# A perceiver layer on one core: the opening of its cross attention, with the query weights prepared a head at a time

## The chip, the core and the metric

The kernel runs on one core of a Trainium2 chip. The core's engines work side by side, each through its own list of instructions in order: TensorE (PE in the profile; PEld are its weight loads), VectorE (DVE), ScalarE (ACT), GpSimd (POOL), and SyncE (SP), whose list here holds almost only DMA transfers. They wait for one another by semaphores. The metric is the device time of one execution in microseconds.

## The reference

One perceiver layer works on a latent array `x` of 32 sequences of 64 tokens with 512 features. It adds three blocks: a cross attention to a context of 32 x 1601 x 512, a causal self attention, and a feed-forward block with ternary weights. Only the opening of the cross attention is touched here:

```python
xn = _rmsnorm(_layernorm(x), rms_scale)              # 2048 tokens x 512
q = jnp.einsum('BTD,NDH->BTNH', xn, q_w)             # 4 heads of 128
q = _apply_rope(q, q_pos) * HEAD_DIM ** (-0.5)       # rotary positions
...
logits = jnp.einsum('BTKGH,BSKH->BKGTS', q, k)
masked = jnp.where(mem_mask[:, None, None, None, :], logits, MASK_FILL)
```

The mask marks which context rows are used. How many rows matter differs by sequence, and the kernel finds that out at run time.

## The kernel before

**Queries without a normalised x.** The kernel never forms `xn`. The weights are scaled by `1 + rms_scale` and their mean over the input features is taken off, which does the layernorm's centring; the tokens' deviations enter only after the product, as a factor per token. So `query` (L231) multiplies the raw, transposed tokens with these centred weights, and `rotate_query` (L237 to L242) multiplies by cosine and sine tables that already hold each token's inverse deviation. The 2048 tokens are taken in four groups of 512, named 0 to 3, and each group has four heads: 16 queries, named here q(group, head).

**The steps for one group.** `fetch_raw` (L194) brings the tokens row by row and `fetch_wide` (L189) brings them transposed. `spread_of` (L200, L201) takes mean and variance of 128 rows on DVE, four times; `deviations` (L207 on DVE, L208 on POOL) makes the inverse deviation. `diagonals` (L215, ACT) writes it on a diagonal; `tables` spreads it over all partitions with one matmul called rb (L224) and makes the cosine and sine tables from it (L226, L227, DVE). `query` is four float32 matmuls of 128 x 512, which the profile lists as eight records. `rotate_query` copies the two halves of the result crosswise (L237, L238, ACT) and makes two products and a sum on DVE (L240, L241, L242). L240 waits for the copies, though it reads only PSUM and a table. The copies have two buffers, so a head's copies wait for L242 of the head two before. The temporary that L240 writes is a single one, so L240 waits for L242 of the head before.

**PSUM.** A query's result lies in one of four banks. Heads 0 and 2 share one pair of banks and heads 1 and 3 the other, so that q(g+1, h) takes the bank that q(g, h) had, and may start only when L240 of that head has read it.

**Weights.** `wo` (1 MB) first holds the query weights, arranged by input chunk: `wo[:, c]` is chunk c of all four heads. They come in two transfers (L289). Four matmuls of 128 x 512 (wmean, L326) give the mean over the input features of all 512 output columns, and four DVE instructions (L346), one for each chunk, scale and centre them.

**Ranking.** Between these the kernel counts which blocks of the context each sequence uses (count, L308, and L315), ranks the sequences by need (L328 to L341, DVE), and places them in a fixed order by two small matmuls (placed, L343 and L344). L353 to L358 write the order and a flag as integers (`ints`). All engines load the flag and branch on it; the transfers of context rows (`nat`, L453) and of transposed context (`ct`, L465) are addressed by the order.

**Order.** `keep_busy(n)` (L284) issues n matmuls whose result nobody reads. At the end of each block `in_order` ties every engine's instructions to the order in which the Python code issued them, SP's transfers too. So what stands ahead in an engine's list holds up all behind it.

**Behind the branch.** `cross_last` runs groups 1 to 3 through `query_steps`; between the queries of group 2 it projects the first sequences' keys and values (kvp, L523). Everything after that (attention by pairs of sequences, self attention, feed-forward) is the same code in both kernels.

## Time and profile before

| | us |
|---|---|
| median of three runs | 894.86 (894.26 to 896.26) |
| the profiled execution | 895.05 |
| its span | 892.2 |
| PE busy in the span | 881.8 (99%) |
| DVE, ACT, POOL busy | 627.4, 377.3, 67.1 |
| first query starts | 11.43 |
| first rb matmul starts | 21.84 |
| fifth query starts | 27.13 |
| first kvp matmul starts | 45.23 |

Rows of the timeline read: start, length, engine, line, operation, tiles out and in, shape, the number of records merged, and in brackets the idle time before them and what ended it. A float32 matmul is two records for PE. Where neighbouring records overlap, the distance between their starts (the pitch) is what one costs.

### The profile page before, as it was taken

Reading aid. Unit: us, or ns where it says so; the run is one execution under the profiler, and the core shown is the slowest. Engines: PE = TensorE matmul, PEld = TensorE weight load, DVE = VectorE, ACT = ScalarE, POOL = GpSimd, SP = SyncE. Lnnn points to the kernel's source line nnn. Section 1 sums busy time; section 2 is a strip of 40 time slices with the busy share of each in tenths; the row PEclk is TensorE's granted clock in tenths of the full one; section 3 lists DMA queues with packets and bytes.
Section 4 is the critical chain, followed back from the end, with each engine's and each line's share of the span. In section 5 each row is a group of like instructions: output and inputs, shape, how many; then the busy total and the mean of one; then the engine's idle time right before and its main releaser. Section 6 shows DMA issues by size and latency. Waiting matters only on the chain.

```text
span 892.2 us, 12926 instructions
## 1 busy us (share of the span) xinstructions
PE 881.8 (99%) x4536; PEld 636.5 (71%) x4536; DVE 627.4 (70%) x1198; ACT 377.3 (42%) x811; POOL 67.1 (8%) x79
## 2 busy tenths in 40 slices
PE   9999999999999999999999999999999999999997
PEld 4456777777778767667666766676668778788885
DVE  5975656455655671588789988986866886876864
ACT  2554545555455441222232323224654554555550
POOL 0110111111101100000000000000001000010000
PEclk9999999999999999999999999999999999999999
DMA  7975798775685343011101101100000020010101
GB/s 259 329 251 179 230 258 259 220 257 157 191 259 160 108 148 116 1 48 34 39 26 47 45 27 37 48 12 1 1 1 1 1 47 1 12 37 1 34 14 53
DMA packets 58723, 88.05 MB, mean 99 GB/s; under 512 B 10516, under 2 KB 30872, under 8 KB 58264
## 3 DMA queue, kind: packets, MB, share of 16 engines
q1 hardware_dynamic: 57888, 86.58, 31.6%
q8 instruction: 38, 0.62, 0.3%
q10 hardware_dynamic: 760, 0.55, 0.2%
q14 instruction: 37, 0.30, 0.1%
HBM read 78.72 MB, written 4.19 MB: 93 GB/s over the span
## 4 chain that ended last, share of the span: by engine, by line
PE 95%; DVE 3%; ACT 1%; issue 0%; POOL 0%; ACTq 0%; POOLq 0%
PE y L1533 14%; PE kvp L523 13%; PE fh L1179 12%; PE aV L1268 6%; PE aWQ L1256 6%; PE q L231 6%; PE aWK L1256 6%; PE aout L1377 6%; PE xo L649 6%; PE lgp L565 3%; PE enc L633 3%; PE sc L1311 2%; PE po L1363 2%; PE pt L618 2%; PE aptp L1350 1%; PE ftp L1168 1%
## 5 line engine op out<-in xcount | busy, mean ns | idle before, releaser
L523 PE MATMUL kvp<-wkv,ct 128*128 128x256 f32 x576 | 134.7, 379 | 0.0
L523 PEld LDWEIGHTS kvp<-wkv,ct 128*128 128x128 f32 x576 | 107.0, 190 | 21.6 <-issue 8.8
L1533 PE MATMUL y<-wp,hTh 128*128 128x512 f32 x236 | 94.5, 400 | 0.4 <-DVE xres L1510 0.4
L1533 PE MATMUL y<-wp,hTl 128*128 128x512 f32 x236 | 92.8, 393 | 0.0
L1179 PE MATMUL fh<-fxh,wf 128*128 128x512 f32 x256 | 72.2, 403 | 1.2 <-DVE xres L1380 0.8
L1187 ACT ACTIVATE bank<-fh 128x512 f32<-128x512 f32 x64 | 38.2, 597 | 76.6 <-PE fh L1179 76.4
L1179 PE MATMUL fh<-fxl,wf 128*128 128x512 f32 x256 | 70.5, 397 | 0.0
L530 ACT ACTIVATE kv<-kvp,rstd 128x256 f32<-128x256 f32 x72 | 34.0, 473 | 84.2 <-PE kvp L523 84.2
L572 DVE CUSTOM_DVE_ANT_0 pr<-lgp,bias 128x384 f32<-128x384 f32 (+6 forms) x64 | 28.5, 458 | 46.9 <-PE lgp L565 46.6
L1377 PE MATMUL aout<-bank,aoT 128*128 128x512 f32 x128 | 59.0, 604 | 0.0
L1528 DVE SCALAR_TENSOR_TENSOR hTl<-bank,lnw,hTh 128x512 fp32r<-128x512 f32 x59 | 44.1, 751 | 21.0 <-ACT hTh L1527 20.9
L649 PE MATMUL xo<-wo,encT 128*128 128x512 f32 x128 | 57.8, 594 | 0.2 <-ACT encT L642 0.2
L231 PE MATMUL q<-xres,wo 128*128 128x512 f32 x128 | 56.4, 593 | 0.6 <-DVE wo L346 0.6
L1179 PEld LDWEIGHTS fh<-fxh,wf 128*128 128x128 f32 x256 | 46.6, 188 | 14.1 <-DVE xres L1380 1.6
L1179 PEld LDWEIGHTS fh<-fxl,wf 128*128 128x128 f32 x256 | 48.2, 188 | 11.2
L1533 PEld LDWEIGHTS y<-wp,hTh 128*128 128x128 f32 x236 | 44.3, 188 | 14.0 <-DVE xres L1510 3.4
L1195 DVE TENSOR_TENSOR sums<-sums,bank 128x512 f32<-128x512 f32 x56 | 38.5, 687 | 19.7 <-ACT bank L1187 19.7
L1533 PEld LDWEIGHTS y<-wp,hTl 128*128 128x128 f32 x236 | 44.5, 188 | 9.9
L1333 ACT ACTIVATE s<-s 128x1024 f32<-128x1024 f32 x15 | 15.9, 1059 | 84.3 <-DVE s L1326 84.3
L1268 PE MATMUL aV<-bank,axT 128*128 128x512 f32 x112 | 51.5, 602 | 0.0
L1256 PEld LDWEIGHTS aWQ<-axT,bank 128*128 128x128 f32 x224 | 42.6, 190 | 11.8 <-issue 6.7
L1355 ACT COPY wo<-aptp 64x256 f32<-64x256 f32 x64 | 23.3, 365 | 64.8 <-PE aptp L1350 47.6
(176 smaller groups left out, 1564.0 us busy)
## 6 DMA issues: line engine op xcount, KB each, us to landing
nat<-in_ctx_dram SPq DMA_DIRECT2D x64, 256.0 KB, 4.7
ct<-in_ctxT_dram SPq DMA_DIRECT2D x7, 768.0 KB, 4.5
xres<-in_x_dram SPq DMA_DIRECT2D x8, 512.0 KB, 6.1
xres<-in_x_dram SPq DMA_DIRECT2D x32, 128.0 KB, 5.0
qs<-bank SPq DMA_DIRECT2D x32, 128.0 KB, 3.8
raw_g<-in_W_fcT_dram SPq DMA_DIRECT2D x16, 256.0 KB, 4.4
raw_g<-in_W_projT_dram SPq DMA_DIRECT2D x16, 256.0 KB, 3.5
raw_q<-in_W_fcT_dram SPq DMA_DIRECT2D x16, 256.0 KB, 2.9
```

Source lines behind the costliest of these rows:

```text
L231: nc.tensor.matmul(ps, wq[:, c, h, :], wide(g)[:, c], start=(c == 0), stop=(c == DC - 1))
L523: nc.tensor.matmul(ps.rearrange("p k h -> p (k h)"), cts[p][:, c, j * P : (j + 1) * P], wkv[:, c].rearrange("p k h -> p (k h)"), start=(c ...
L530: nc.scalar.activation(kvs[p][:, j], ps, AF.Copy, scale=rstds[p][:, j : j + 1])
L649: nc.tensor.matmul(o, encT[:, h].rearrange("p s t -> p (s t)"), wo[:, h, :], start=(h == 0), stop=(h == NH - 1),)
L1179: nc.tensor.matmul(ps, wf[:, c, cols], part[:, c, :], start=(i == 0 and c == 0), stop=(i == 1 and c == DC - 1),)
L1187: nc.scalar.activation(g, ps, AF.Gelu)
L1195: nc.vector.tensor_tensor(sums[:, 0], so_far[0], g, ALU.add)
L1256: nc.tensor.matmul(ps[:, m, :], ws[w][:, c, (m0 + m) * P : (m0 + m + 1) * P], xT[:, c, :], start=(c == 0), stop=(c == DC - 1),)
L1268: nc.tensor.matmul(ps, xT[:, c, i * P : (i + 1) * P], ws["WV"][:, c, :], start=(c == 0), stop=(c == DC - 1),)
L1377: nc.tensor.matmul(ps, oT[:, c, :], ws["WO"][:, c, :], start=(c == 0), stop=(c == DC - 1))
L1528: nc.vector.scalar_tensor_tensor(lo, g, w, hi.bitcast(F32), ALU.mult, ALU.subtract)
L1533: nc.tensor.matmul(y, part[:, t, :], wp[:, c, :], start=(c == 0 and i == 0), stop=(c == FC - 1 and i == 1),)
```

## The change

The query weights are arranged by head: `wo[:, h]` holds all four chunks of head h. They arrive in three transfers (head 0, head 1, heads 2 and 3) with the transposed tokens of group 0 behind the first. The mean is taken for one head at a time, four matmuls of 128 x 128, and a head is centred by four DVE instructions of 128 x 128. Head 0 is done right after the counts, ahead of the ranking; heads 1 and 2 after q(0, 0) and the ranking's end; head 3 after q(0, 1). The filler matmuls go from 5 + 4 to 5 + 1 + 2.

The transposed tokens of group 1 are fetched at the start, instead of behind q(0, 1). The statistics of group 1 move on DVE from ahead of the tables of group 0 to behind the rotation of q(0, 1), and their diagonals on ACT from behind the copies of q(0, 1) to behind those of q(0, 2). The tables of group 1 (its rb and L226, L227) move across the branch: they were made ahead of q(1, 0) and are now made behind q(1, 2), and on DVE behind the statistics of group 2. The rotations of q(1, 0), q(1, 1) and q(1, 2) then follow together. Groups 2 and 3 keep their order.

```diff
-    wq = wo.rearrange("p c (h k) -> p c h k", h=NH)
+    wq = wo.rearrange("p h (c k) -> p c h k", c=DC)
...
         for g in range(1, GROUPS):
             more = g + 1 < GROUPS
+            waiting = []
             for h in range(NH):
-                q = query(g, h, psq(h, f"q_{g}_{h}"))
-                if h == 0 and g > 1:
+                waiting.append((h, query(g, h, psq(h, f"q_{g}_{h}"))))
+                if h == (2 if g == 1 else 0):
                     tables(g, qrot, psr(f"rb_{g}"))
-                rotate_query(g, h, q)
+                if h >= 2 or g > 1:
+                    for k, q in waiting:
+                        rotate_query(g, k, q)
+                    waiting.clear()
                 if more and h < 2:
                     spread_of(g + 1, 2 * h)
...
         nc.scalar.dma_start(scale1, a["rms"])
-        for k in (0, 2):
-            nc.sync.dma_start(wo[:, k : k + 2], a["wq"][:, k : k + 2])
-        keep_busy(5)
+        nc.sync.dma_start(wo[:, 0], a["wq"][:, 0])
+        fetch_wide(0, [nc.sync, nc.sync])
+        nc.sync.dma_start(wo[:, 1], a["wq"][:, 1])
+        nc.sync.dma_start(wo[:, 2:], a["wq"][:, 2:])
+        fetch_raw(0)
+        fetch_wide(1, [nc.sync])
+        qrot = fetch_rotations(r1)
+        nc.sync.dma_start(wkv, a["wkv"])
...
-        fetch_wide(0, [nc.sync, nc.sync])
-        fetch_raw(0)
-        qrot = fetch_rotations(r1)
-        nc.sync.dma_start(wkv, a["wkv"])
+        heads = [ps_q[h % 2].tile([P, GQ], F32, tag="q", name=f"q_0_{h}") for h in range(NH)]
+
+        def averaged(h):
+            ps = ps_b.tile([P, HD], F32, tag="b", name=f"wmean_{h}")
+            for c in range(DC):
+                nc.tensor.matmul(
+                    ps, each[:, c], wq[:, c, h], start=(c == 0), stop=(c == DC - 1)
+                )
+            return ps
+
+        def centre(h, ps):
+            for c in range(DC):
+                nc.vector.scalar_tensor_tensor(
+                    wq[:, c, h], wq[:, c, h], scale1[:, c : c + 1], ps, ALU.mult, ALU.subtract
+                )
+
+        keep_busy(5)
...
-        keep_busy(4)
-        wmean = ps_b.tile([P, D], F32, tag="b", name="wmean")
-        for c in range(DC):
-            nc.tensor.matmul(wmean, each[:, c], wo[:, c], start=(c == 0), stop=(c == DC - 1))
+        keep_busy(1)
+        centre(0, averaged(0))
+        keep_busy(2)
         need = r1.tile([B, B], F32, name="need")
...
         nc.vector.tensor_scalar(here, table[:, 2], rank, None, ALU.is_equal)
+        query(0, 0, heads[0])
         placed = ps_r.tile([P, 2, B], F32, tag="r", name="placed")
...
-        for c in range(DC):
-            nc.vector.scalar_tensor_tensor(
-                wo[:, c], wo[:, c], scale1[:, c : c + 1], wmean, ALU.mult, ALU.subtract
-            )
-        heads = [ps_q[h % 2].tile([P, GQ], F32, tag="q", name=f"q_0_{h}") for h in range(NH)]
-        query(0, 0, heads[0])
...
         nc.vector.tensor_copy(ints[:, B:], fit)
+        means = [averaged(h) for h in (1, 2)]
+        for h in (1, 2):
+            centre(h, means[h - 1])
+        query(0, 1, heads[1])
+        mean = averaged(3)
         for k in range(4):
             spread_of(0, k)
         deviations(0)
         diagonals(0)
+        centre(3, mean)
         for c in range(DC):
             nc.scalar.activation(wkv[:, c], wkv[:, c], AF.Copy, scale=scale1[:, c : c + 1])
-        query(0, 1, heads[1])
         fetch_raw(1)
-        fetch_wide(1, [nc.sync])
-        for k in range(4):
-            spread_of(1, k)
-        deviations(1)
         query(0, 2, heads[2])
         tables(0, qrot, ps_b.tile([P, GQ], F32, tag="b", name="rb_0"))
         query(0, 3, heads[3])
         for h in range(NH):
             rotate_query(0, h, heads[h])
             if h == 1:
+                for k in range(4):
+                    spread_of(1, k)
+                deviations(1)
+            if h == 2:
                 diagonals(1)
-        tables(1, qrot, ps_b.tile([P, GQ], F32, tag="b", name="rb_1"))
...
-    arrays["wq"] = given["L0_xattn_q_w"].reshape(NH, DC, P, HD).transpose(2, 1, 0, 3).reshape(P, DC, D)
+    arrays["wq"] = given["L0_xattn_q_w"].reshape(NH, DC, P, HD).transpose(2, 0, 1, 3).reshape(P, NH, D)
```

## The prediction

> **What bounds the kernel now.** I read the page's busy shares and its chain of waits first, then PE's timeline over the opening, then ACT's and DVE's.

> ```profile
> PE 881.8 (99%) x4536; PEld 636.5 (71%) x4536; DVE 627.4 (70%) x1198; ACT 377.3 (42%) x811; POOL 67.1 (8%) x79
> ...
> PE 95%; DVE 3%; ACT 1%; issue 0%; POOL 0%; ACTq 0%; POOLq 0%
> ```

> PE is busy for 99% of the span and carries 95% of the chain. So a change in the opening is worth just what it shifts PE's later work.

> ```profile
> 1.06 2.50 PE L284 MATMUL idle<-ones 128*128 128x128 f32 x10 [1.06 <-DVE neghalf L96]
> ...
> 5.02 2.08 PE L284 MATMUL idle<-ones 128*128 128x128 f32 x8
> 6.89 3.70 PE L326 MATMUL wmean<-wo,each 128*128 128x512 f32 x8
> ...
> 11.43 10.57 PE L231 MATMUL q<-xres,wo 128*128 128x512 f32 x24 [0.64 <-DVE wo L346]
> 21.84 1.02 PE L224 MATMUL rb<-xres,ones 128*128 128x512 f32 x2
> ...
> 26.16 1.13 PE L224 MATMUL rb<-xres,ones 128*128 128x512 f32 x2
> 27.13 17.40 PE L231 MATMUL q<-xres,wo 128*128 128x512 f32 x40
> 44.37 1.02 PE L224 MATMUL rb<-xres,ones 128*128 128x512 f32 x2
> 45.23 1.89 PE L523 MATMUL kvp<-wkv,ct 128*128 128x256 f32 x8
> ```

> From 11.43 on PE never stops. A query costs 3.44 us (17.40 / 5 less the last record's tail), an rb 0.86. The five queries from 27.13 run without a gap, so q(2,0) starts at 27.13 + 4 x 3.44 = 40.9. I use the start of the first kvp, 45.23, as the mark: behind it the PE list is the same in both kernels, and PE has no large idle to absorb a shift.

> What a 128-wide float32 record costs on PE is not seen in the opening, where idle records follow each other at 0.213 us; a later stretch shows it:

> ```profile
> 288.53 0.61 PE L565 MATMUL lgp<-kT,qs 128*128 128x128 f32 x4
> 288.97 1.89 PE L633 MATMUL enc<-pT,kv 128*128 128x256 f32 x8
> ```

> Four records take 288.97 - 288.53 = 0.44, so 0.110 each: PE ran the idle records at half speed, and was at full speed when wmean began (eight 512-wide records at 0.43).

> The handshake around a rotation, ACT and then DVE:

> ```profile
> 18.50 1.28 ACT L215 ACTIVATE xres<-ident,qrs 128x128 f32<-128x128 f32 x4 [14.36 <-POOL qrs L208]
> 19.68 1.69 ACT L364 ACTIVATE wkv<-wkv,scale 128x256 f32<-128x256 f32 x4
> 21.39 0.58 ACT L237 COPY qt<-q 64x512 f32<-64x512 f32 x1
> 21.98 0.58 ACT L238 COPY qt<-q 64x512 f32<-64x512 f32 x1
> ```

> ```profile
> 34.34 0.68 DVE L240 TENSOR_TENSOR xres<-q,xres 128x512 f32<-128x512 f32 x1
> 34.94 0.68 DVE L241 TENSOR_TENSOR qt<-qt,xres 128x512 f32<-128x512 f32 x1
> 35.65 0.69 DVE L242 TENSOR_TENSOR bank<-xres,qt 128x512 f32<-128x512 f32 x1
> 36.26 0.69 DVE L200 BATCH_NORM_STATS2 stats_q<-xres 128x6 f32<-128x512 f32 x1
> ```

> A rotation takes DVE 1.92 us before other work (34.34 to 36.26), and 2.12 before another rotation (24.82 to 26.94 in group 0). q(1,0) was read by 35.0; its bank is asked for at 40.9, so q(2,0) has 5.9 us to spare.

> **Step 1: the first query.** The counts stay, and one filler starts at 5.02. Its two records (0.375 and 0.213 apart, as now) put head 0's mean at 5.61. Its weights, 256 KB issued at 1.20, should have landed: 145 KB took 2.3 us and 512 KB took 4.6. Eight records at the half-speed 0.213, the last one lasting 0.42, give the mean at 7.5. Then comes an instruction that no row shows: a 128-wide scaling on DVE. Bounds: the 32-wide L331 at 0.18 us, and the 512-wide L346 at 0.74; on the line between them 0.29. PE started 0.06 after L346's first one, so q(0,0) starts at 7.5 + 0.3 + 0.06, say 7.9, against 11.43. Its tokens hold it no longer: they now stand behind 0.4 MB; before, the first half landed at 8.8 behind 1.2 MB, at 1.35 us for 512 KB, so about 6.5 now and the second half about 8.0, which is first used at 9.7. The ranking, now behind head 0's scaling, ends near 10.9 (need to here took 2.4), before q(0,0) is through at 11.4; nobody waits for it. **Gain 3.5.**

> **Step 2: what moves in among the queries.** Three means of eight records at 0.110 are 2.65, and placed 0.2 (it lay under a wait before). Three queries with what lies between took 10.41 (11.43 to 21.84). So rb(0) starts at 7.9 + 10.41 + 2.65 + 0.2 = 21.2, **0.65 earlier** than 21.84. It needs diagonals(0). On DVE the integers end at 12.4, eight scalings follow at an estimated 0.26 (pitch of L346 0.66; of a 32-wide instruction 0.10 to 0.2) with mean 1 ready at 12.6, then statistics 14.9 to 18.2 (13.88 to 17.19 took 3.31), POOL and ACT 2.6 more: 20.8. Slack 0.4; the other heads' scalings are done before their queries. The four 128-wide means cost 32 x 0.110 = 3.5, as much as the wide ones (8 x 0.43); the loss is only that 24 of these records now lie behind the first query.

> [...]

> **Step 3: group 1's tables, and DVE.** Count from T = start of rb(0). PE: q(0,3) and three queries of group 1, then rb(1), then q(1,3) want q(2,0) at T + 19.06 (as before, 40.9 - 21.84, rb(1) only moved). Now DVE. L226 starts at T + 1.05 (rb at 65.87 to L226 at 66.92), the rotation of q(0,0) at T + 2.3, of q(0,1) at T + 4.4, group 1's statistics at T + 6.3, L207 at T + 9.65, rotation of q(0,2) at T + 9.7 (q(1,2) wants that bank at T + 11.3: 0.9 to spare). Then a gap: diagonals(1) stand on ACT ahead of q(0,3)'s copies and wait for POOL. From L207: 1.31 to ACT (17.19 to 18.50), 1.18 for the diagonals, 1.17 for the copies, so rotation of q(0,3) at T + 13.35, where DVE was free at T + 11.8. Then statistics of group 2 from T + 15.3 (3.39), tables(1) 1.21, and L240 of q(1,0) from T + 19.9 to T + 20.55. q(2,0), which takes its bank, starts at T + 20.6: **PE stands still for 1.55 us**, and all queries, kvp and the rest queue behind it. Restarting costs 0.1 (first to second record 0.53 instead of 0.43). Next late is rb(2): q(1,2)'s copies wait for L242 of q(1,0) at T + 21.9, copies and diagonals(2) end at T + 24.4, rb(2) is wanted at T + 24.1: 0.3, and 0.1 for the restart. From there DVE has 13 us of work for 21 us of PE's and catches up.

> [...]

> **Queues.** SP issues one transfer more (0.43 of issue, all issued by 6, in front of nothing waiting). wide(1) goes out with the opening; wkv lands near 17 instead of 14.2, used at 20.7. raw(1) still waits for the statistics of group 0, now at 16.6 and 18.2 (before 15.38 and 16.97); it stands in front of the context rows, so the earlier integers start nothing earlier. raw(2) waits for the statistics of group 1: 29.2 and 30.9 (before 23.25 and 24.72), landing by 37, while DVE takes its first half at 36.5 and second at 38.1. wide(2) behind it goes at 31.7 and lands 7.1 later, 38.8, wanted at 40.3. ct lands near 41, wanted at 46.6. POOL only has its power instructions later.

> **Sum.** -0.65 + 1.55 + 0.1 + 0.3 + 0.1 = +1.4 us. Against the profiled execution (892.2 of span, 895.05) that is 896.45; it lies 0.2 above the median of 894.86. I take **896.4**. 0.2% (1.8 us) is about what measurement can tell from no change here.

> **Rivals.**
> *The ledger holds but for small sizes*, forecast: 895.3 to 897.5. Chance 0.48, a third of it above the 896.65 where slower begins.
> *The narrow scaling is dear* (slower). At 0.66 pitch instead of 0.26, eight of them push the statistics, diagonals(0) and rb(0) by 3.2 less the slack of 0.4, and the first query by 0.45: rb(0) near 24.1, net +4.3, 899.3. It decides from a pitch of 0.36, where it costs 0.4 and the total passes 1.8. For it: the instruction reads PSUM and is unmeasured; against: L331 is short. Chance 0.17.
> *PE cools in the stall* (slower): eight records of q(2,0) at 0.86 instead of 0.43, +3.4, 899.8. For it: the idle records show that a half speed exists; against: the 0.64 wait ahead of 11.43 left full speed. Chance 0.07.
> *No stall* (not slower): if ACT's copies of q(0,3) do not stand behind the diagonals, DVE gains 1.55 and q(2,0) starts in time: 895.05 - 0.65 + 0.1 = 894.4. With the first query at 7.4 and PE already at full speed, 893.5 to 894. For it: the gap hangs on one order on ACT; against: that order is written out. Chance 0.2, a third of it faster by 0.2%.
> *The early tokens do not come early*: first half at 8.8 as before, q(0,0) at 8.9, +1.0, 897.4. The rest, 0.08, holds this, late transfers of raw(2) and what I do not see.

> **Chances.** Faster 0.07 + 0.03 = 0.10. Within: 0.32 + 0.13 + 0.01 = 0.46. Slower 0.16 + 0.17 + 0.07 + 0.04 = 0.44. The range takes in no stall and most of the dear scaling: 894.3 to 898.9.

> **What would show it.** After: q(0,0) near 7.9; 128-wide wmean records 0.11 apart behind it; rb(0) near 21.2; a wait of PE before the ninth query, 1 to 2 us, ended by DVE L240; ACT's copies of q(0,3) waiting behind diagonals; first kvp near 46.6. It is wrong if PE shows no such wait, if rb(0) waits for ACT long, or if records behind the wait are 0.86 apart.

## The result, and the profile after

| | before | after |
|---|---|---|
| median | 894.93 us (894.26 to 896.31, 9 executions) | 898.12 us (896.83 to 899.27, 9 executions) |
| the profiled execution, and its span | 895.05, 892.2 | 898.62, 897.0 |
| first query starts | 11.43 | 8.00 |
| first rb starts | 21.84 | 21.46 |
| q(2,0) starts | 40.89 (27.13 + 4 x 3.44) | 42.49 |
| first kvp starts (the mark) | 45.23 | 47.32 |

The ratio is 1.0029, with a 95% interval of 1.0021 to 1.0037: the changed kernel is 0.29% slower (by the two medians alone 0.36%). 896.4 was forecast. The result lies inside the range and on the side on which the forecast lay, but the rise is 3.2 us and not 1.5. The mark accounts for 2.1 of it; where the rest comes from is half of what follows. The two spans differ by 4.8 us, but the last instruction that computes (a DVE sum ahead of the output transfer) starts only 3.77 later, at 890.05 instead of 886.28, and the times of the two profiled executions differ by 3.57; the spans are therefore not compared below.

From the page of the changed kernel, the chain of waits by engine:

```profile
PE 94%; DVE 3%; ACT 1%; issue 1%; POOL 0%; ACTq 0%; POOLq 0%
```

PE is still the bound (busy 884.0 us of 897.0), and the chain has a new percent of "issue": a wait of PE in which the page names no releaser. PE's timeline of the changed kernel over the opening shows it:

```profile
5.61 1.91 PE L313 MATMUL wmean<-wo,each 128*128 128x128 f32 x8
...
8.00 3.67 PE L231 MATMUL q<-xres,wo 128*128 128x512 f32 x8
...
11.81 2.05 PE L313 MATMUL wmean<-wo,each 128*128 128x128 f32 x16
...
21.46 1.02 PE L224 MATMUL rb<-xres,ones 128*128 128x512 f32 x2
22.32 13.90 PE L231 MATMUL q<-xres,wo 128*128 128x512 f32 x32
...
36.91 3.60 PE L231 MATMUL q<-xres,wo 128*128 128x512 f32 x8
42.49 3.67 PE L231 MATMUL q<-xres,wo 128*128 128x512 f32 x8 [1.98 <-issue]
46.36 1.12 PE L224 MATMUL rb<-xres,ones 128*128 128x512 f32 x2 [0.20 <-ACT xres L215]
47.32 1.89 PE L544 MATMUL kvp<-wkv,ct 128*128 128x256 f32 x8
```

The first query is 3.4 us earlier, but 16 and then 8 narrow mean records now lie behind it, 0.11 apart, and only 0.4 us is left at rb(0). Five queries and an rb further on PE stands still for 1.98 us ahead of q(2,0). The bracket says "issue"; which instruction it is comes from DVE's timeline:

```profile
34.97 0.69 DVE L240 TENSOR_TENSOR xres<-q,xres 128x512 f32<-128x512 f32 x1 [1.72 <-ACT qt L238]
...
37.09 0.69 DVE L200 BATCH_NORM_STATS2 stats_q<-xres 128x6 f32<-128x512 f32 x1
...
41.71 0.68 DVE L240 TENSOR_TENSOR xres<-q,xres 128x512 f32<-128x512 f32 x1
```

L240 at 41.71 is that of q(1,0), whose bank q(2,0) takes; it ends at 42.39, and PE starts 0.1 later. Ahead of it DVE lost 1.72 us waiting for ACT's copies of q(0,3). ACT's timeline has the reason:

```profile
32.46 1.28 ACT L215 ACTIVATE xres<-ident,qrs 128x128 f32<-128x128 f32 x4 [5.37 <-POOL qrs L208]
33.77 0.58 ACT L237 COPY qt<-q 64x512 f32<-64x512 f32 x1
```

The diagonals of group 1 stand ahead of the copies and wait for POOL, as the prediction said.

**The part that was not in the sum.** Behind the mark the two PE lists keep a distance of 2.1 us, up to the fh matmuls (a product of the feed-forward block) at 651.21 (649.08 before). Then the distance grows to 3.8 (659.19 against 655.43) and stays there to the end. PE's timeline there, first of the kernel before:

```profile
647.17 1.98 PE L1151 MATMUL spread<-side,pick 4*128 4x512 f32 x4
649.08 1.20 PE L1179 MATMUL fh<-fxh,wf 128*128 128x512 f32 x4
...
651.05 3.60 PE L1377 MATMUL aout<-bank,aoT 128*128 128x512 f32 x8
655.43 1.19 PE L1179 MATMUL fh<-fxh,wf 128*128 128x512 f32 x4 [0.79 <-DVE xres L1380]
```

and of the changed kernel:

```profile
649.30 1.98 PE L1172 MATMUL spread<-side,pick 4*128 4x512 f32 x4
651.21 1.19 PE L1200 MATMUL fh<-fxh,wf 128*128 128x512 f32 x4
...
653.67 4.73 PE L1398 MATMUL aout<-bank,aoT 128*128 128x512 f32 x8
659.19 1.20 PE L1200 MATMUL fh<-fxh,wf 128*128 128x512 f32 x4 [0.78 <-DVE xres L1401]
```

The aout row (the output product of the self attention) took 3.60 in the kernel before and takes 4.73 here. The spread row holds matmuls that use only 4 rows (4*128, 4x512; the fh and aout rows have 128*128). The view by stretches of 2 us (stretch and its length, then the busy time and instructions of PE, PEld, DVE, ACT and POOL, then the granted clock of PE, the DMA share and GB/s), again of the changed kernel:

```profile
652.00:654.00 2.00, 2.00 (x7) 1.63 (x6) 1.65 (x3) 1.04 (x3) 0.00 (x0) 0.63 0.00 0
654.00:656.00 2.00, 2.00 (x3) 0.68 (x3) 0.67 (x3) 1.14 (x2) 0.54 (x1) 0.51 0.00 0
```

PE is busy all the time, but was granted half clock from 652.54 to 655.95, for 3.41 us (the stretches before and behind have 1.00), which costs the 1.6 us by which the distance grows. The kernel before has 1.00 in each of these stretches. So two things had to be explained: the mark, and a half-clock stretch 600 us behind everything that the change touches.

The second matters for reading all times below. Executions of one kernel fall into groups some 1.6 us apart. That these are the executions with no such stretch, with one and with two is read from the profiled ones and from the size of the step; it was not seen in each. The nine of the changed kernel are 896.83, 896.98 and 897.19, then 897.51, then five from 898.12 to 899.27: by this reading its median is a time with a half-clock stretch, while most executions of the kernel before have none.

### The profile page after: what moved, and what is told of

Read it like the earlier page. It is cut to its first block, busy times and chain, and to the rows that moved or that the text cites. A ratio compares the mean times of both kernels' runs of the same rounds, so it can differ in the third digit from the quotient of the medians.

```text
span 897.0 us, 12987 instructions
## 1 busy us (share of the span) xinstructions
PE 884.0 (99%) x4558; PEld 639.4 (71%) x4558; DVE 629.3 (70%) x1210; ACT 377.3 (42%) x811; POOL 67.3 (8%) x79
## 4 chain that ended last, share of the span: by engine, by line
PE 94%; DVE 3%; ACT 1%; issue 1%; POOL 0%; ACTq 0%; POOLq 0%
PE y L1554 13%; PE kvp L544 13%; PE fh L1200 12%; PE aV L1289 6%; PE aWQ L1277 6%; PE aWK L1277 6%; PE aout L1398 6%; PE xo L670 6%; PE q L231 6%; PE lgp L586 3%; PE enc L654 3%; PE sc L1332 2%; PE po L1384 2%; PE pt L639 2%; PE aptp L1371 1%; PE ftp L1189 1%
## 5 line engine op out<-in xcount | busy, mean ns | idle before, releaser
L593 DVE CUSTOM_DVE_ANT_0 pr<-lgp,bias 128x384 f32<-128x384 f32 (+6 forms) x64 | 28.5, 458 | 46.9 <-PE lgp L586 46.6
L231 PE MATMUL q<-xres,wo 128*128 128x512 f32 x128 | 56.9, 593 | 2.0 <-issue 2.0
L1200 PEld LDWEIGHTS fh<-fxh,wf 128*128 128x128 f32 x256 | 46.6, 188 | 14.1 <-DVE xres L1401 1.6
L1200 PEld LDWEIGHTS fh<-fxl,wf 128*128 128x128 f32 x256 | 48.5, 189 | 11.3
L1277 PEld LDWEIGHTS aWQ<-axT,bank 128*128 128x128 f32 x224 | 42.6, 190 | 11.8 <-issue 6.7
L1277 PE MATMUL aWK<-axT,bank 128*128 128x256 f32 x224 | 50.6, 379 | 0.0
```

Of the source, the lines that this page charges most:

```text
L231: nc.tensor.matmul(ps, wq[:, c, h, :], wide(g)[:, c], start=(c == 0), stop=(c == DC - 1))
L1200: nc.tensor.matmul(ps, wf[:, c, cols], part[:, c, :], start=(i == 0 and c == 0), stop=(i == 1 and c == DC - 1),)
L1277: nc.tensor.matmul(ps[:, m, :], ws[w][:, c, (m0 + m) * P : (m0 + m + 1) * P], xT[:, c, :], start=(c == 0), stop=(c == DC - 1),)
```

## The experiments

All kernels compute the whole result. They ran in three sets, each set on one chip beside its own executions of the kernel before: medians 895.59 (first set, 30 executions), 895.34 (second, 32) and 895.45 (third, 27). Ratios go by these.

### The kernel before, once more

> The kernel before, run again as if it were a change, so that the mean clock of each of its executions is listed. Theory 'clock windows': 1.1 us of the 3.2 us lost lie behind the first kvp, in one window of 3.41 us at half clock (652.54 to 655.95 in the profile after); whether a window falls so depends on a phase the kernel does not set, so some executions of the kernel before must show it too: mean clock near 0.997 with times 1.7 us above those at 0.999. Rival 'the change slows the later code': every execution of the kernel before stands at 0.999, and its times do not go with its clock.

Measured: 895.0 us (12 executions), ratio 0.9993 (0.9985 to 1.0002). Ten lie between 893.9 and 895.7; the two with a mean clock of 0.997 instead of 0.999 took 896.3 and 896.6. So, going by time and mean clock together, for no profile shows one, the kernel before has executions with a slower clock too, only fewer. In its profiled execution the first query started at 10.72, rb(0) at 21.13 and the first kvp at 44.89: 0.7, 0.7 and 0.3 earlier than in the execution that the prediction was worked out from. One profile fixes the times of this opening to a few tenths only.

### Statistics of group 1 back ahead of the tables

```diff
+        for k in range(4):
+            spread_of(1, k)
+        deviations(1)
         for h in range(NH):
             rotate_query(0, h, heads[h])
             if h == 1:
-                for k in range(4):
-                    spread_of(1, k)
-                deviations(1)
-            if h == 2:
                 diagonals(1)
```

> The changed kernel, with group 1's statistics back ahead of the tables of group 0 and its diagonals behind the copies of q(0,1), as before; rb(1) stays behind three queries. Theory 'late statistics': the wait ahead of q(2,0) (2.14 us) goes. The second half of group 1's rows landed at 22.66 in the profile after, so tables of group 0 move from 22.5 to about 24.4 and q(1,0) waits about 0.6; first kvp at 45.3 instead of 47.3, time 2.1 below the changed kernel, level with the kernel before. Rival 'the narrow means cost': the time stays within 0.5 us of the changed kernel, and the kvp comes no earlier than 46.5.

Measured: 896.55 us (12 executions), ratio 1.0010 (1.0002 to 1.0019). PE's timeline:

```profile
26.55 10.54 PE L231 MATMUL q<-xres,wo 128*128 128x512 f32 x24 [0.78 <-DVE xres L240]
...
37.78 7.03 PE L231 MATMUL q<-xres,wo 128*128 128x512 f32 x16
```

There is no wait ahead of q(2,0): 16 records follow 37.78 without a gap. A smaller wait of 0.78 stands at q(1,0) instead, because DVE twice waits 0.7 for the rows of group 1 to arrive before it can take their statistics, and the rotation of q(0,0) comes late (25.61). The mark is 45.51. So the place of the statistics on DVE, with the diagonals that follow them, makes the 2-us wait. The median, expected level with the kernel before, is 0.1% above it, and one thing here is not explained: seven of the twelve executions lie 1.5 us above the others at mean clocks of 0.996 and 0.997, although the profiled one (895.06) holds no wait near 2 us. The rows of group 1 may arrive later in those; no run shows it.

### Only ACT's order changed

```diff
-            if h == 2:
+            if h == 3:
                 diagonals(1)
```

> The changed kernel, with group 1's diagonals on ACT behind the copies of q(0,3) instead of ahead of them. If ACT's order makes 1.7 us of DVE's lateness, the rotation of q(0,3) starts at 33.4 instead of 34.97, the wait ahead of q(2,0) falls from 2.14 to about 0.5, first kvp at 45.7: 1.6 below the changed kernel, 0.5 above the kernel before. If the statistics on DVE alone set it, the wait stays above 1.5 and the time within 0.6 us of the changed kernel.

Measured: 895.36 us (12 executions), ratio 1.0003 (0.9994 to 1.0011). PE's timeline, the two rows that answer to 42.49 and 47.32 above:

```profile
40.64 3.67 PE L231 MATMUL q<-xres,wo 128*128 128x512 f32 x8 [0.41 <-PE q L231]
...
45.47 1.89 PE L544 MATMUL kvp<-wkv,ct 128*128 128x256 f32 x8
```

and DVE's row of L240 of q(0,3), 34.97 above:

```profile
33.11 0.69 DVE L240 TENSOR_TENSOR xres<-q,xres 128x512 f32<-128x512 f32 x1
```

It starts earlier and has no wait ahead of it. PE's wait falls from 1.98 to 0.41 and the mark from 47.32 to 45.47. Of these 1.85 us, 0.29 is not the edit's: rb(0) is that much earlier in this execution (21.17). Counted from rb(0), one line of order on ACT, an engine that is 42% busy, is worth 1.56 us, and what is left of the slow-down lies within what can be measured.

### The order of group 1 alone, with the old front

The new `query_steps` and the new places of the statistics, diagonals and tables of group 1, put into the kernel before.

```diff
-        for k in range(4):
-            spread_of(1, k)
-        deviations(1)
...
             if h == 1:
+                for k in range(4):
+                    spread_of(1, k)
+                deviations(1)
+            if h == 2:
                 diagonals(1)
-        tables(1, qrot, ps_b.tile([P, GQ], F32, tag="b", name="rb_1"))
```

> The kernel before with the new order of group 1 alone: its statistics behind the rotation of q(0,1), its diagonals behind that of q(0,2), its tables behind three queries; weights, means and opening as before. Theory 'late statistics': the same chain from rb(0) (21.84) to q(2,0) takes 21.03 us, so q(2,0) starts at 42.9 with 2.1 us of waiting, first kvp 47.7, 2.5 us slower than the kernel before. Rival 'the opening costs': no wait longer than 0.5, first kvp within 0.5 us of 45.2, the same time as before.

Measured: 898.31 us (6 executions), ratio 1.0031 (1.0019 to 1.0043). PE's timeline:

```profile
42.69 3.67 PE L231 MATMUL q<-xres,wo 128*128 128x512 f32 x8 [1.91 <-issue]
...
47.53 1.67 PE L527 MATMUL kvp<-wkv,ct 128*128 128x256 f32 x7
```

The whole loss is there without the head-wise weights: from rb(0), at 21.30 here, to the mark it is 26.23 us, against 23.39 and 23.76 in the two profiles of the kernel before.

### The head-wise front alone

The reverse: the new front, with group 1 handled as before.

```diff
+        for k in range(4):
+            spread_of(1, k)
+        deviations(1)
         for h in range(NH):
             rotate_query(0, h, heads[h])
             if h == 1:
-                for k in range(4):
-                    spread_of(1, k)
-                deviations(1)
-            if h == 2:
                 diagonals(1)
+        tables(1, qrot, ps_b.tile([P, GQ], F32, tag="b", name="rb_1"))
...
-                if h == (2 if g == 1 else 0):
+                if h == 0 and g > 1:
                     tables(g, qrot, psr(f"rb_{g}"))
```

> The front of the change alone (query weights a head at a time, counts ahead of the ranking), with the statistics, diagonals and tables of group 1 where they were before, ahead of the branch. Theory: rb(0) near 21.4, 0.4 earlier than before; then rb(1), wanted at 25.7, waits for the diagonals of group 1, which POOL and ACT have ready near 26.9, so the fifth query starts near 28.1 instead of 27.1 and the first kvp near 46.0, 0.8 later than before: ratio 1.0005 to 1.0012. Rival (the head-wise front is a gain that the new order of group 1 throws away): rb(1) does not wait, kvp near 44.8, median 0.4 below before.

Measured: 896.13 us (11 executions), ratio 1.0009 (1.0000 to 1.0018). PE's timeline:

```profile
7.92 3.67 PE L231 MATMUL q<-xres,wo 128*128 128x512 f32 x8 [0.67 <-DMA xres<-in_xT_dram]
...
26.50 1.13 PE L224 MATMUL rb<-xres,ones 128*128 128x512 f32 x2 [0.67 <-ACT xres L215]
```

The front by itself is no gain: rb(1) waits 0.67 for the diagonals of group 1, and the mark is 45.55. A first query 3 us earlier moves rb(0) hardly at all. Over the eleven profiles of kernels with the new front, rb(0) starts between 20.93 and 21.82, on average at 21.33; the three profiles with the old front have 21.84, 21.13 and 21.30, on average 21.42.

### Filling the wait with matmuls that nobody reads

```diff
+            if g == 2:
+                fill = psr("fill")
+                for _ in range(8):
+                    nc.tensor.matmul(fill[:, :P], ones, ones, start=True, stop=True)
             for h in range(NH):
                 waiting.append((h, query(g, h, psq(h, f"q_{g}_{h}"))))
```

> The changed kernel with eight 128-wide filler matmuls put in front of q(2,0), where PE stands still for 2.1 us; nobody reads their result, the computation is the same. Theory A (the standing still itself makes the half-clock windows of 3.41 us, later in the execution, more frequent): the wait is filled, q(2,0) still starts near 42.5 and the first kvp near 47.3, but executions with a mean clock of 0.997 or less fall from 7 in 9 to about the 2 in 12 of the kernel before, and the median goes to about 897.2. Theory B (the 2 us of shift set the frequency, by where the late matmuls lie against the windows, idleness or not): the same starts and the same share of low clocks as in the changed kernel, median about 898.1.

Measured: 896.8 us (10 executions), ratio 1.0021 (1.0012 to 1.0030). PE's timeline:

```profile
39.82 1.95 PE L252 MATMUL fill<-ones 128*128 128x128 f32 x16
42.00 3.67 PE L231 MATMUL q<-xres,wo 128*128 128x512 f32 x8 [0.23 <-issue]
```

q(2,0) starts as far behind rb(0) as in the changed kernel (21.07 against 21.03): the bank is free no sooner. Yet eight of ten executions lie between 896.4 and 897.1, and only two 1.5 us above, at 898.2 and 898.7. The changed kernel has five of nine there. That is near the share that theory A expects, and the standing still would have a second price, paid by the clock. It is not proved by this: 2 of 10 against 5 of 9 are few, the two ratios' intervals overlap, by the measure that was named beforehand (a mean clock of 0.997 or less) it is 4 of 10 against 7 of 9, and the kernel with the statistics ahead of the tables has seven of twelve in the upper group without a wait near 2 us. The profile of the next run shows that the clock can fall at this wait.

### Where the clock falls: at the wait, or at the 4-row matmuls

```diff
-        pick = fw.tile([4, 2, P], F32, name="pick")
+        pick = fw.tile([P, 2, P], F32, name="pick")
...
+            nc.gpsimd.memset(side, 0.0)
             nc.vector.tensor_copy(side[:4], ps[:4])
...
-                    nc.tensor.matmul(ps, pick[:, k, :], side[:4], start=True, stop=True)
+                    nc.tensor.matmul(ps, pick[:, k, :], side, start=True, stop=True)
```

> The changed kernel with the spread matmuls near 649 us (four records of 512 columns, of which only 4 rows held data) widened to all 128 rows, the added rows zero, so that the result is the same. Theory C (a window filled by matmuls of 4 rows counts as idle, and the next one is given half clock): no half-clock window behind the spread, PE's shift against the kernel before stays at +2.1 us through 659, executions with a mean clock of 0.997 or less become rare, median about 896.9 to 897.2, that is 1.6 lower less what the wider operand costs (a memset on an engine off the path: nothing). Theory D (the window falls there by chance or for another reason): the half-clock window stays in the executions and the median is within 0.5 of the changed kernel's.

Measured: 897.11 us (11 executions), ratio 1.0023 (1.0014 to 1.0032). By the times alone it was inconclusive: five of eleven executions still lie 1.5 us above the rest. The profiled execution, one of them (898.39), showed why. Its PE timeline, and then its stretches of 2 us:

```profile
42.85 5.37 PE L231 MATMUL q<-xres,wo 128*128 128x512 f32 x8 [1.99 <-issue]
```

```profile
42.00:44.00 2.00, 1.15 (x2) 0.64 (x3) 1.97 (x4) 0.00 (x0) 0.11 (x1) 0.82 1.01 390
44.00:46.00 2.00, 2.00 (x4) 0.69 (x3) 1.86 (x4) 1.76 (x5) 0.00 (x0) 0.50 1.06 324
```

Eight records that take 3.67 behind the same wait in the changed kernel's profile take 5.37 here: PE got half clock from 43.28 to 46.69, right behind the wait. This is the rival "PE cools in the stall", in an execution of a kernel whose opening is that of the changed one. So the changed kernel can lose the clock at two places, and this run could close only the later one. The later one is told apart below, on a base without the wait.

### Half the statistics ahead of the tables

```diff
+        for k in (0, 1):
+            spread_of(1, k)
         for h in range(NH):
             rotate_query(0, h, heads[h])
             if h == 1:
-                for k in range(4):
+                for k in (2, 3):
                     spread_of(1, k)
                 deviations(1)
-            if h == 2:
+            if h == 3:
                 diagonals(1)
```

> The changed kernel with the statistics of group 1 cut in two: the first two of the four go ahead of the tables of group 0, where DVE waits for rb(0) anyway; the other two stay behind the rotation of q(0,1), and the diagonals of group 1 go behind ACT's copies of q(0,3). Theory (the shift of the mark is DVE's lateness alone, made of 3.3 us of statistics in the rotations and 1.7 us of gap by ACT's order): with half the statistics out and the gap gone, L240 of q(1,0) starts about 3.4 us earlier than in the changed kernel (near 38.3), PE does not wait before q(2,0), rb(0) stays at 21.5, the first kvp is at 44.8, 0.4 ahead of the kernel before, and the median is 0 to 0.5 below it (ratio 0.9995 to 1.000). Rival (something behind the mark, such as the late transfers of group 2's tokens, takes the gain): a new wait of PE before rb(2) or kvp of over 0.5 us, and a median over 895.5.

Measured: 894.34 us (11 executions), ratio 0.9990 (0.9981 to 0.9999). PE's timeline, the queries on both sides of q(2,0) and the mark:

```profile
36.52 7.03 PE L231 MATMUL q<-xres,wo 128*128 128x512 f32 x16
...
44.24 1.89 PE L546 MATMUL kvp<-wkv,ct 128*128 128x256 f32 x8
```

q(2,0) follows q(1,3) without a gap, and from rb(0) at 21.07 to the mark PE never waits: 23.17 us, against 23.39 and 23.76 in the two profiles of the kernel before and 25.86 in that of the changed one. L240 of q(1,0) starts at 38.16, as expected; the gain is larger than expected. The same kernel on another chip:

> The same kernel as the one with the statistics of group 1 cut in two, on another chip and as the base of the three kernels run with it. Theory (its mark is 0.4 to 0.9 ahead of the kernel before and nothing takes it back): ratio 0.999 again, interval within 0.998 to 1.000, about 2 in 11 executions some 1.5 us above the rest. If the earlier 1.0 us was that chip's chance: ratio 0.9997 to 1.0003.

Measured: 894.22 us (11 executions), ratio 0.9988 (0.9979 to 0.9997). The gain of 0.1% is there twice. It is 1.0 and 1.2 us by the medians, but 0.6 by the marks (44.24 and 44.37, against 45.23 and 44.89). The two profiled executions of the kernel before, 895.05 and 894.78, lie 0.3 to 0.7 below the medians of their kernel in these sets; in which part of it the others lose that was not shown.

### The spread matmuls, wide, twice, and both

On the kernel with the statistics cut in two: the 128-row spread of above; the 4-row spread issued twice; the 128-row spread issued twice.

```diff
+                    for _ in range(2):
-                    nc.tensor.matmul(ps, pick[:, k, :], side[:4], start=True, stop=True)
+                        nc.tensor.matmul(ps, pick[:, k, :], side[:4], start=True, stop=True)
```

> The kernel with the statistics cut in two, and the spread matmuls near 646 us widened from 4 rows to 128 (zeros in the rows added, the same result). Theory C (4-row matmuls count as idleness of PE and now and then bring a half-clock window): the 2 in 11 executions that lie 1.5 us above the rest disappear, the rest stay at 894.3, median 0 to 0.2 lower. Theory D (those executions have another cause): their share stays near 2 in 11.

> The kernel with the statistics cut in two and the spread matmuls of 4 rows issued twice (the second writes the same values over the first; the result is the same): 3.96 us of 4-row work in a row instead of 1.98. Theory C: whatever the phase, one window of 3.41 us now holds at least 2.0 us of it, so a half-clock window follows in nearly every execution, and the time is 894.3 + 2.0 + 1.6 = 897.9, in some executions 899.5 with two such windows. Theory D: 896.3, as with 128 rows, and no half-clock window behind the spread.

> The kernel with the statistics cut in two and the spread matmuls widened to 128 rows and issued twice: the same 3.96 us of PE time as with 4 rows, with all rows active. Theories C and D both: 894.3 + 2.0 = 896.3 and no half-clock window; against the 4-row kernel C expects 1.6 less, D the same. If the extra matmuls lie beside a wait that PE has anyway, both kernels gain back the same amount.

| kernel | median, us | executions, and their spread | ratio to the kernel before |
|---|---|---|---|
| 4 rows, once | 894.22 | 11: ten from 893.64 to 894.59, one 895.78 | 0.9988 (0.9979 to 0.9997) |
| 128 rows, once | 894.02 | 11: 893.72 to 894.84 | 0.9985 (0.9976 to 0.9994) |
| 4 rows, twice | 899.16 | 5: 898.94 to 899.20 | 1.0044 (1.0030 to 1.0058) |
| 128 rows, twice | 895.92 | 11: 895.41 to 896.51 | 1.0006 (0.9997 to 1.0015) |

The second pass costs 1.9 us with 128 rows, about its own time (from the first spread record to the second set of fh matmuls 4.46 us instead of 2.75), and 4.9 with 4 rows. The stretches of 2 us of the 4-row kernel, issued twice:

```profile
650.00:652.00 2.00, 2.00 (x5) 1.22 (x5) 1.18 (x4) 0.59 (x1) 0.54 (x1) 0.50 0.00 0
652.00:654.00 2.00, 2.00 (x6) 1.60 (x5) 0.00 (x0) 0.00 (x0) 0.00 (x0) 0.50 0.00 0
654.00:656.00 2.00, 2.00 (x4) 0.89 (x3) 0.00 (x0) 1.23 (x2) 0.00 (x0) 0.50 0.00 0
```

and of the 128-row kernel, issued twice:

```profile
650.00:652.00 2.00, 2.00 (x9) 1.47 (x8) 1.48 (x4) 0.59 (x1) 0.31 (x1) 1.00 0.00 0
```

## Why the prediction was right or wrong

**The bound.** Right: PE carries 94% of the chain and the mark moves the end. Behind the mark the lists kept their distance (2.1) until the clock fell.

**Step 1, the first query.** Right: 7.9 forecast, 8.00 measured; over the eleven profiles with the new front it is 7.45 to 8.36, on average 7.87, so that the agreement to 0.1 in one profile is partly luck. The scaling that no row had shown has a pitch close to 0.26 (four in 1.12, eight in 2.16), as the line between two rows gave; so the dear scaling, which had a chance of 0.17, did not come. The tokens were the weak point: their first half landed at 7.87, not 6.5. The page shows no loss by it in this execution, but in five of the eleven profiles with the new front the first query waits for that transfer, 0.6 to 1.3 us (0.67 in the front alone).

**Step 2, what moves in among the queries.** The price of the narrow means was right, 0.11 a record. The gain at rb(0) was over-sized: 0.65 forecast, 0.38 in this pair of profiles, 0.1 as an average over all. The first error is 0.1 us in the start of the first query and 0.2 in the length of the stretch. The second is that the sum was made against one execution whose rb(0), at 21.84, was the latest of three.

**Step 3, the wait.** The mechanism was right in each link: DVE's L240 of q(1,0) ends it, ACT's copies stand behind the diagonals, and rb(2) waits a little afterwards. The size was not: 1.55 was forecast, q(2,0) starts 2.14 later than the two rb and five queries ahead of it need. Counted from rb(0), PE wanted the bank at 18.89, not 19.06; the rotation of q(0,3) began at 13.51, not 13.35; statistics of group 2 at 15.63, not 15.3, since a rotation took 2.12 on DVE here where 1.92 or so was counted; and the end is at 21.03, not 20.6. Four small errors, all to the same side, make the wait 0.6 longer. The first only lengthens the wait; the other three put q(2,0) 0.43 later behind rb(0). With 0.38 instead of 0.65 from step 2 they make the mark 2.09 later instead of 1.4. That the wait belongs to the order and not to the front is shown by the order alone (mark 47.53). Of the 2.09, ACT's list carries 1.56, counted from rb(0), as the late diagonals show; so the rival "No stall", which hung on that list, had the right condition, but a wait of 0.41 would have been left.

**The rival that was put too low.** "PE cools in the stall" had a chance of 0.07 and a price of 3.4. A half-clock stretch is the part of the result for which the sum has no term; that the wait would cost none of the clock was assumed. The argument against it, that a wait of 0.64 had left full speed, was no bound for one of 2 us. Where it was seen, its price was 1.7 (5.37 instead of 3.67), not 3.4: the half clock lasted 3.41 us there (43.28 to 46.69), and not for all eight records. And it is a matter of chance by execution: the profile of the changed kernel shows full speed behind the wait and the loss elsewhere; the kernel with the wide spread shows it at the wait, which was 1.99 us there. How often the changed kernel itself loses the clock at the one place and at the other was not shown. The 4-row matmuls, where its profile shows the loss, were in no sum and no rival.

**Queues.** Between rb(0) and the mark no engine of the changed kernel waits for a transfer, as forecast.

## What to carry to other kernels

When statistics or tables move to a later place in an engine's list, count what stands behind them on every engine: here moving one call on ACT took back as much of the mark as moving all the statistics did (marks of 45.47 and 45.51), and cutting the statistics in two as well turned 0.3% of loss into 0.1% of gain. Getting the first query out early is worth only what is left at the next common point, and that needs more than one profile where the opening depends on when transfers land. A wait of PE of about 2 us (1.99 in the profile that lost the clock by it), or as much time in matmuls of 4 rows (1.91), should be priced twice, going by these runs: its length, and a share of the 1.6 to 1.7 us that the clock cost.

## What the runs showed of the hardware that was not expected

**The clock fell at whole multiples of 3.413 us.** The traces' records of the granted clock have three half-clock stretches in mid-kernel: 652.54 to 655.95 in the changed kernel, 43.28 to 46.69 in the wide spread, both of 3.41 us (3.413 in the record of the first), and 649.49 to 656.32 in the 4-row spread issued twice, twice that. Each starts a whole number of 3.413 us behind the moment at which the execution reached full clock: 652.54 - 7.42 is 189.0 of them in the changed kernel, 43.28 - 5.73 is 11.0, 649.49 - 4.37 is 189.0. So does the fall behind the last matmul: 891.14 - 7.09 is 259.0 in the kernel before, 894.88 - 7.42 is 260.0 in the changed one. A window, below, is a stretch of 3.413 us counted from that first moment. The moment differs from execution to execution (4.37, 5.73, 7.09 and 7.42 us in these four profiles), so the same wait lies across a boundary in one and inside a window in another: the changed kernel's 1.98 us are cut by the boundary at 41.55 into 1.05 and 0.93, the 1.99 of the wide spread lie in one window (39.87 to 43.28). If all phases are equally frequent, an estimate from these lengths has the whole wait in one window in (3.41 - 1.99) / 3.41 = 0.42 of the executions; with the wide spread five of eleven lie in the upper group. This fits a kernel's times falling into groups.

**At about 1.9 us in one window the clock fell in some profiles and not in others.** Counted by such windows, the clock fell behind 1.91 us of 4-row matmuls (changed kernel), 1.99 of idleness (wide spread) and 3.09 of 4-row matmuls (spread twice). It did not fall behind 1.88 of idleness (order alone), nor behind 1.91 of 4-row matmuls in three other kernels (statistics early, wait filled, statistics halved for the second time), nor, at full clock, behind less in any profile. What decides at 1.91 was not found.

**The second half-clock window came behind less.** With the 4-row spread issued twice the second half-clock window (652.90 to 656.32) followed a window with 1.0 us of 4-row work, while 1.05 us of idleness in a window at full clock was followed by a clock of 1.00 in the changed kernel. One trace shows this; the times of all five executions fit it.

**The 128-row spread was not slower.** Widening the spread from 4 to 128 rows left its stretch no longer: from its first record to the second set of fh matmuls 2.94 us with 4 rows (changed kernel), 2.75 with 128 (the halved statistics with the wide spread).
